# A GRU, a convolution and an expert layer on one core: the state h turned by VectorE in place of TensorE

## The chip, the cores and the metric

The kernel runs on one core of a Trainium2 chip. The metric is the device time of one execution in microseconds; a run's time is the median of several executions. A profile is one further execution with the hardware profiler on; its own time stands beside its span below.

## What is computed

The reference, cut to what matters. x is (128, 64, 512): 128 sequences (B), 64 steps (T), 512 features (D); the condition is (128, 512).

```python
def cell(h, x):                                  # GRU: 64 steps, one after the other
    gi = x @ W_ih + b_ih                         # 512 -> 3 * 512
    gh = h @ W_hh + b_hh
    i_r, i_z, i_n = split(gi, 3); h_r, h_z, h_n = split(gh, 3)
    r = sigmoid(i_r + h_r); z = sigmoid(i_z + h_z)
    n = tanh(i_n + r * h_n)
    return (1 - z) * n + z * h

hs = scan(cell, cond, x)
x = x + hs @ (ternary(weight) * scale).T + bias  # "ffn", ternary weights
y = causal_depthwise_conv(x, taps=cond) + b      # 64 taps per feature
x = x + y_experts(y) + shared_expert(y)          # top 6 of 64 experts, capacity 64
```

All inputs and outputs are float32.

## The kernel before

The program has two halves. The first, which the change is in, walks through the 64 steps of the GRU (some 1230 of the 2465 us); the second makes the convolution, the shared expert and the routed experts, and is left as it is.

The batch lies on the 128 partitions: the state `h`, the gates and `n` are tiles of 128 x 512. For the products TensorE needs h with the features on the partitions, so each step turns h: `turned_up` (L412) makes four 128x128 transposes on TensorE against an identity into one PSUM tile, `pst`. The full-precision product is made of three products on reduced operands: `split_h` (L419) cuts the low bits of the turned h (`hcut`, L344, VectorE), copies that (`hh`, L424, ScalarE), takes the rest (`hl`, L350, VectorE) and a mixture of both (`hs`, L351, VectorE). `split_x` (L367) does the same to the next step's input x, but there the rest, `xl`, is taken by GpSimd (L350 on POOL), followed on GpSimd by the addition of the ffn's bias (L286). Weights are split once, at the start.

The loop (L569) goes over t. In each turn TensorE makes, in an order that a scheduler settles when the kernel is built:

- nine groups of four products with hh, hl and hs: the gates' state parts (`psx`, `psy`: r; `psw`, `psz`: n; `psa`, `psb`: z),
- two groups of the ffn of the step before (`psf`, hh and hl with the ternary weights),
- six groups of the next step's input parts of n and r (`psw`, `psz`, `psx`, `psy`),
- the four transposes of the new h (L416),
- three groups of the next step's input part of z (`psa`, `psb`).

VectorE and ScalarE make the gates meanwhile (`cell_r`, `cell_n`, `cell_z`, L471 to L506; L506 writes the new h), then VectorE gathers the next step's input part of n (`gi`, L391 and L392), and then comes the cut of the turned h. Every engine executes its own queue in order. The gates r and z share one tile, `rz`, of the pool `el0` with one buffer; so do hcut, hh, hl and hs each.

Steps 0 to 3 are special: their turned h is also stored, since the ternary weights are ready only in step `LATE` = 4 (`ternary`, L448), and the ffn of these four steps is made up for in steps 6, 9, 12 and 15 (`late_ffn`, L551: it cuts a loaded h, and adds two groups to TensorE's turn). In step 4 the ternary weights are made on VectorE (L466, L467), after the gates.

`next_inputs` (L530) is where the turn is asked for:

```python
            if t in postponed:
                late_ffn(postponed[t])
            turned = turned_up(h)
            ...
            if t > 0:
                pieces = split_h(turned)
            input_gate(t + 1, 1)
```

After the loop the last h is turned once more by `turned_up`, for the last ffn.

Of the kernel before, what the change touches and what calls it, by code (L numbers as in the profile page):

```python
# [8 lines left out]
F32 = mybir.dt.float32  # L9
# [10 lines left out]
P = 128  # L20
B = 128
T = 64
D = 512
KD = D // P
# [21 lines left out]
def adaln_ffn_kernel(  # L46
# [22 lines left out]
    nc = tc.nc  # L69
# [139 lines left out]
    with (  # L209
# [46 lines left out]
        LATE = 4  # L256
# [38 lines left out]
        h = el0.tile([P, D], F32, name="h")  # L295
# [31 lines left out]
        def banks(c):  # L327
            pool = ps_gh if c == 1 else ps_gi
            return [pool.tile([P, D], F32, name=n) for n in BANKS[c]]
# [13 lines left out]
        def masked(dst, src):  # L343
            return nc.vector.tensor_scalar(  # L344
                dst.bitcast(I32), src.bitcast(I32), LOW, None, ALU.bitwise_and
            )

        def low_parts(engine, lo, mix, full, cut):

            i = engine.tensor_sub(lo, full, cut)  # L350
            nc.vector.scalar_tensor_tensor(mix, lo.bitcast(F32), -SPLIT, cut, ALU.mult, ALU.add)  # L351
            return i
# [26 lines left out]
        def input_gate(t, c):  # L379

            xh, xl, xs = parts_of[t]
            wh, wl, ws = wih[c]
            a, b = banks(c)
            products(a, xh, wh, start=True)
            products(a, xl, wl, stop=c == 2 or c in PLAIN.get(t, ()))
            products(b, xs, ws, start=True, stop=c == 2)
            if c != 2:
                gis[t, c] = a, b
                return
            g = el0.tile([P, D], F32, name="gi")  # L390
            nc.vector.scalar_tensor_tensor(g, a, WHOLE, bin_, ALU.mult, ALU.add)  # L391
            nc.vector.tensor_add(g, b, g)  # L392
            gis[t, c] = g
# [18 lines left out]
        def turned_up(src):  # L412
            ps = ps_f.tile([P, D], F32, name="pst")
            ps = ps.rearrange("p (k b) -> p k b", k=KD)
            for k in range(KD):
                nc.tensor.transpose(ps[:, k, :], src[:, k * P : (k + 1) * P], ident)  # L416
            return ps

        def split_h(ps, mixed=True):  # L419

            cut = el0.tile([P, KD, B], F32, name="hcut")
            hh, hl, hs = (el0.tile([P, KD, B], F32R, name=f"h{n}") for n in "hls")
            masked(cut, ps)
            nc.scalar.copy(hh, cut)  # L424
            if mixed:
                low_parts(nc.vector, hl, hs, ps, cut)
            else:
                nc.vector.tensor_sub(hl, ps, cut)
            return hh, hl, hs
# [80 lines left out]
        for c in (0, 2, 1):  # L510
            a, b = banks(c)
# [18 lines left out]
        def next_inputs(t):  # L530

            if t > 0:
                input_gate(t + 1, 2)
                input_gate(t + 1, 0)
            else:
                input_gate(1, 0)
                input_gate(1, 2)
            if t in postponed:
                late_ffn(postponed[t])
            turned = turned_up(h)  # L540
            hT = pieces = None
            if t < LATE:
                hT = io0.tile([P, KD, B], F32, name="xn")
                nc.scalar.copy(hT, turned)
                nc.sync.dma_start(out=htd[t], in_=hT.rearrange("p k b -> p (k b)"))
# [3 lines that stand above are left out]
            return pieces, hT  # L549

        def late_ffn(t):  # L551

            hh, hl = (el0.tile([P, KD, B], F32R, name=f"h{n}") for n in "hl")
            cut = el0.tile([P, KD, B], F32, name="hcut")
            full = hts.pop(t).rearrange("p (k b) -> p k b", k=KD)
            masked(cut, full)
            nc.scalar.copy(hh, cut)
            nc.vector.tensor_sub(hl, full, cut)
            ffn(t, (hh, hl))

        split_x(1)
        for c in (0, 2, 1):
            convert(raw_i[c], wih[c], stm)
        load_xt(2)
        pieces, hT = next_inputs(0)
        convert(raw_h[0], whh[0], stm)
        stage.close()

        for t in range(1, T):  # L569
# [28 lines left out]
            if t + 1 < T:  # L598
                pieces, hT = next_inputs(t)
            if t in (1, 2):  # L600
                c = 3 - t
# [38 lines left out]
        with tc.issue_after(grouped[-1].ins):  # L640
            turned = turned_up(h)
        early.append(conv_group(0, 3, ps_gi.tile([P, D], F32, name="psz")))
        pieces = split_h(turned, False)
        with tc.issue_after(grouped[-1].ins):
            ffn(T - 1, pieces)
# [1010 lines left out]
```

## Time and profile before

| what | value |
| --- | --- |
| median of 3 runs | 2467.7 us (2464.25 to 2468.32) |
| profiled execution: its own time | 2466.93 us |
| profiled execution: span from the first to the last instruction | 2465.2 us |
| granted TensorE clock | 0.998 |
| TensorE busy | 2450.6 us (99%) |
| VectorE busy | 1547.5 us (63%) |
| ScalarE busy | 462.6 us (19%) |
| GpSimd busy | 447.2 us (18%) |
| in the recurrence, 320 to 1215 us: TensorE, VectorE busy | 895.0 of 895.0 us, 642.2 us |

In the profile PE is TensorE, PEld its loading of weights, DVE VectorE, ACT ScalarE, POOL GpSimd, SP SyncE. A line such as L344 is the line of the kernel; helpers record all their callers' work under their own line, so hcut, xcut and the cuts of the weights are all L344. In a timeline the columns are start and length in us, then what ran; an "x4" is four instructions merged into one row, and brackets give the engine's idle time ahead of it and who ended it. In a list of groups the columns behind the first bar are the sum in us and the mean of one in ns, behind the second the idle time ahead of them. Matmuls overlap: a row's length is more than the distance to the next row.

### The profile page before, as it was taken

The page shows a single profiled execution, that of the slowest core. Times are in us where ns is not written, and L with a number is a line of the kernel's source. Part 1 is how long each engine was busy: PE and PEld are TensorE (multiplying, and loading weights), DVE is VectorE, ACT ScalarE, POOL GpSimd, SP SyncE. Part 2 cuts the span into 40 slices and gives each one's busy share as a digit, 9 for nine tenths or more (in the row PEclk, how much of TensorE's full clock was granted, in tenths as well). Part 3 has the DMA queues.
Part 4 walks back from the last instruction along what each step waited for, and adds up shares of the span by engine and source line. Part 5 has one row for each costly group of instructions (what it writes and reads, how often), then busy time and mean ns, then how long its engine had stood idle before and what let it go on. Part 6 is the DMA issues. An engine that isn't in the chain of part 4 may idle for free.

```text
span 2465.2 us, 32121 instructions
## 1 busy us (share of the span) xinstructions
PE 2450.6 (99%) x12317; PEld 1886.5 (77%) x12317; DVE 1547.5 (63%) x3073; ACT 462.6 (19%) x847; POOL 447.2 (18%) x468
## 2 busy tenths in 40 slices
PE   9999999999999999999999999999999999999999
PEld 5788888888888888888896678888876666666667
DVE  8877777777777777677686566666664333443344
ACT  5211111111111111111122222222211111111111
POOL 1122221112111211221220000000011222222220
PEclk9999999999999999999999999999999999999999
DMA  5244443233222222222498212222368999899961
GB/s 182 74 87 80 82 80 62 58 68 63 60 54 59 59 52 55 61 56 43 111 336 295 39 25 40 56 58 62 103 173 288 299 299 311 267 334 292 290 172 44
DMA packets 464456, 322.33 MB, mean 131 GB/s; under 512 B 316592, under 2 KB 384176, under 8 KB 462128
## 3 DMA queue, kind: packets, MB, share of 16 engines
q1 hardware_dynamic: 435408, 246.34, 34.8%
q0 software_dynamic: 28896, 73.95, 13.2%
q8 instruction: 97, 1.59, 0.3%
q14 instruction: 55, 0.45, 0.1%
HBM read 233.44 MB, written 92.03 MB: 132 GB/s over the span
## 4 chain that ended last, share of the span: by engine, by line
PE 97%; DVE 1%; issue 1%; DMA 0%; ACT 0%; POOL 0%; DVEq 0%; SPq 0%; ACTq 0%; POOLq 0%
PE psa L333 9%; PE psw L333 9%; PE psx L333 9%; PE psw L815 8%; PE psx L815 8%; PE psz L815 8%; PE psy L333 5%; PE psb L333 5%; PE psf L333 5%; PE psz L333 5%; PE y L815 4%; PE py L1541 3%; PE pg L1515 3%; PE pu L1515 3%; PE y L992 2%; PE psc L191 2%
## 5 line engine op out<-in xcount | busy, mean ns | idle before, releaser
L1525 DVE SCALAR_TENSOR_TENSOR a<-a,rw,pu 128x352 f32<-128x352 f32 x32 | 18.6, 581 | 213.0 <-PE pu L1515 213.0
L351 DVE SCALAR_TENSOR_TENSOR xs<-xl,xcut 128x512 fp32r<-128x512 f32 x63 | 103.4, 1641 | 68.1 <-POOL xl L350 68.1
L344 DVE TENSOR_SCALAR hcut<-pst 128x512 int32<-128x512 int32 x63 | 43.5, 690 | 130.9 <-PE pst L416 128.7
L1097 POOL DMA_DIRECT2D out_dram<-hid x32 | 27.7, 1006 | 449.6 <-issue 333.6
L350 POOL TENSOR_TENSOR xl<-xp,xcut 128x512 fp32r<-128x512 f32 x60 | 83.4, 1391 | 141.9 <-PE psa L333 141.7
L479 ACT ACTIVATE rz<-rz 128x512 f32<-128x512 f32 x64 | 40.5, 633 | 341.6 <-DVE rz L478 341.6
L424 ACT CAST hh<-hcut 128x512 fp32r<-128x512 f32 x63 | 39.2, 622 | 341.9 <-DVE hcut L344 341.9
L268 POOL DMA_DIRECT2D q<-in_x_dram x36 | 19.3, 537 | 419.1 <-DMA out_dram<-q 202.1
L1541 PE MATMUL py<-wd,aeT 128*64 128x512 f32 (+1 forms) x384 | 88.8, 597 | 0.0
L1515 PE MATMUL pg<-wg,xeT 128*64 128x352 f32 x512 | 81.2, 459 | 0.0
L1515 PE MATMUL pu<-wu,xeT 128*64 128x352 f32 x512 | 81.2, 459 | 0.0
L1552 POOL DMA_INDIRECT out_dram<-ys,idxo x32 | 45.5, 1422 | 179.8 <-DMA out_dram<-ys,idxp 161.1
L1552 POOL DMA_INDIRECT out_dram<-ys,idxp x32 | 46.3, 1448 | 174.3 <-DMA out_dram<-ys,idxo 85.1
L268 POOL DMA_DIRECT2D xn<-in_x_dram x28 | 15.0, 536 | 325.6 <-DMA out_dram<-xn 176.2
L333 PE MATMUL psa<-wih1h,xh 128*128 128x512 f32 x252 | 73.9, 414 | 0.0
L1515 PEld LDWEIGHTS pg<-wg,xeT 128*64 128x64 f32 x512 | 36.5, 136 | 47.2 <-issue 46.6
L492 ACT ACTIVATE n<-n 128x512 f32<-128x512 f32 x64 | 40.5, 633 | 165.6 <-DVE n L491 163.2
L855 ACT ACTIVATE g<-psx 128x256 f32<-128x256 f32 x80 | 30.7, 383 | 217.6 <-DVE aT L862 158.5
L333 PE MATMUL psf<-sgn,hl 128*128 128x512 f32 x256 | 70.1, 397 | 0.0
L333 PE MATMUL psf<-sgn,hh 128*128 128x512 f32 x256 | 69.5, 393 | 0.3 <-ACT hh L424 0.3
L333 PE MATMUL psw<-wih2h,xh 128*128 128x512 f32 x252 | 68.7, 395 | 0.0
L333 PE MATMUL psa<-wih1l,xl 128*128 128x512 f32 x252 | 68.6, 394 | 0.0
(404 smaller groups left out, 6183.3 us busy)
## 6 DMA issues: line engine op xcount, KB each, us to landing
wg<-in_w_gate_dram SPq DMA_DIRECT2D x64, 704.0 KB, 12.1
wu<-in_w_up_dram SPq DMA_DIRECT2D x64, 704.0 KB, 12.5
wd<-in_w_down_dram SPq DMA_DIRECT2D x64, 512.0 KB, 9.9
xc<-x1c SPq DMA_DIRECT2D x32, 512.0 KB, 6.6
xp<-in_xT_dram POOLq DMA_DIRECT2D x62, 256.0 KB, 3.0
tab<-hid SPq DMA_DIRECT2D x56, 256.0 KB, 4.3
wd<-in_w_down_dram SPq DMA_DIRECT2D x64, 192.0 KB, 9.8
q<-in_x_dram POOLq DMA_DIRECT2D x36, 256.0 KB, 2.9
```

Source lines behind the costliest of these rows:

```text
L191: i = nc.tensor.matmul(ps[rows, j].rearrange("p h (u t) -> p h u t", u=2), xcs[sl % NCB][:, rows, g * 4 + j], tzs[sl % NCB][:, :, :, g * 4 ...
L333: i = nc.tensor.matmul(ps, lhs[:, k, :], rhs[:, k, :], start=start and k == 0, stop=stop and k == KD - 1, skip_group_check=True,)
L344: return nc.vector.tensor_scalar(dst.bitcast(I32), src.bitcast(I32), LOW, None, ALU.bitwise_and)
L350: i = engine.tensor_sub(lo, full, cut)
L351: nc.vector.scalar_tensor_tensor(mix, lo.bitcast(F32), -SPLIT, cut, ALU.mult, ALU.add)
L479: nc.scalar.activation(r, r, AF.Sigmoid)
L492: nc.scalar.activation(n, n, AF.Tanh)
L815: i = nc.tensor.matmul(ps.rearrange("p (j b) -> p j b", b=P) if len(r.shape) == 3 else ps, lhs(k), r, start=(first and k == 0), stop=(k == ...
L992: nc.tensor.matmul(gu.rearrange("p (j b) -> p j b", b=P), swr[:, k].rearrange("p w n -> p (w n)"), rows[:, k], start=(k == 0), stop=(k == ...
L1515: nc.tensor.matmul(acc[halves[j]], self.xeT[:, k, halves[j]], self.ws[j][which][:, k, :], start=(k == 0), stop=(k == KD - 1),)
L1541: nc.tensor.matmul(py[halves[j]], self.aeT[:n, c, halves[j]], self.ws[j][2][:n, c, :], start=(c == 0), stop=(c == len(ech) - 1),)
L1552: nc.gpsimd.indirect_dma_start(out=out, out_offset=bass.IndirectOffsetOnAxis(ap=(idxp[:CAP] if j == 0 else idxo)[:, q : q + 1], axis=0), i ...
```

## The change

From step 4 on the turn is made by `turned_over` instead of `turned_up`: sixteen VectorE transposes, each of a 32-partition block of h with four blocks of 32 columns, 128 columns apart. Each writes one 32-partition block of the turned tile. The turned h lies in the tile `rz` of the gates (SBUF) instead of `pst` (PSUM). As built, the first transpose stands between L391 and L392 in VectorE's queue and the other fifteen behind L392, ahead of the cut; TensorE's queue is the same but for the four transposes less; in step 4 seven transposes are interleaved with the making of the ternary weights, and xs of the next input stands ahead of the cut. The changed file has 12 lines more from L419 on, so that its line numbers lie 12 higher behind there.

```diff
+        Q = 32
+
+        def turned_over(src):
+
+            dst = el0.tile([P, D], F32, name="rz").rearrange("p (k b) -> p k b", k=KD)
+            rows = src.rearrange("b (k j c) -> b k j c", k=KD, c=Q)
+            for j in range(P // Q):
+                for i in range(B // Q):
+                    own, new = slice(i * Q, (i + 1) * Q), slice(j * Q, (j + 1) * Q)
+                    nc.vector.transpose(dst[new, :, own], rows[own, :, j, :])
+            return dst
+
...
-            turned = turned_up(h)
+            turned = turned_over(h) if t >= LATE else turned_up(h)
```

## The prediction

> **What bounds the kernel now.** I read the page's shares first, then the chain that ended last, then one steady step of the recurrence on each engine, then the waits of the recurrence (320 to 1215 us).
>
> ```profile
> PE 2450.6 (99%) x12317; PEld 1886.5 (77%) x12317; DVE 1547.5 (63%) x3073; ACT 462.6 (19%) x847; POOL 447.2 (18%) x468
> ...
> PE 97%; DVE 1%; issue 1%; DMA 0%; ACT 0%; POOL 0%; DVEq 0%; SPq 0%; ACTq 0%; POOLq 0%
> ```
>
> TensorE is never out of work: less work for it is worth its full time, but only until another engine makes it wait. So the question is how much room the recurrence leaves. One step, TensorE first, then VectorE (start, length, what; in brackets the idle time before):
>
> ```profile
> 1023.95 1.08 PE L333 MATMUL psy<-wih0s,xs 128*128 128x512 f32 x4
> 1024.87 0.60 PE L416 MATMUL pst<-ident,h 128*128 128x128 f32 x4
> 1025.22 1.17 PE L333 MATMUL psa<-wih1h,xh 128*128 128x512 f32 x4
> 1026.23 1.09 PE L333 MATMUL psa<-wih1l,xl 128*128 128x512 f32 x4
> ...
> 1028.07 1.08 PE L333 MATMUL psx<-whh0h,hh 128*128 128x512 f32 x4
> ```
>
> ```profile
> 1021.00 0.69 DVE L506 TENSOR_TENSOR h<-h,n 128x512 f32<-128x512 f32 x1
> 1021.61 0.68 DVE L391 SCALAR_TENSOR_TENSOR gi<-psw,bin 128x512 f32<-128x512 f32 x1
> 1022.40 0.69 DVE L392 TENSOR_TENSOR gi<-psz,gi 128x512 f32<-128x512 f32 x1
> 1025.51 0.69 DVE L344 TENSOR_SCALAR hcut<-pst 128x512 int32<-128x512 int32 x1 [2.42 <-PE pst L416]
> ```
>
> h is ready at 1021.69, but TensorE turns it only at 1024.87, behind the next step's input products: VectorE idles 2.42 us. The first product that needs the turned h (psx, 1028.07) has not to wait. The previous psx began at 1009.20, so a step lasts 18.87 us. Below, times are from that psx.
>
> **The change, part by part.** Step 4 to step 62 are changed: 59 turns; the last one (t = 63) stays.
>
> *Removed:* four transposes of 128x128 per turn. They start 0.35 us before psa, and psa's first group takes 1.01 us where a group usually takes 0.91: 0.45 us of TensorE per step, all on the bounding engine. Without a wait the step would be 18.42 us.
>
> *Added:* sixteen VectorE transposes of 32 partitions x 128 elements. The built order puts the first between the two gi lines and fifteen behind the second, all ahead of the cut. No row shows such an instruction. The nearest is a copy of 128 elements, the next a pair of tiny copies that go to different halves of the partitions:
>
> ```profile
> L1533 DVE COPY aeT<-py 96x128 f32<-96x128 f32 x32 | 8.9, 278 | 0.0
> ...
> L1502 DVE COPY rw<-rows 64x1 f32<-64x1 f32 x64 | 9.1, 143 | 0.5
> ```
>
> The same pair in the timeline, start and length of both together:
>
> ```profile
> 1838.81 0.30 DVE L1502 COPY rw<-rows 64x1 f32<-64x1 f32 x2
> ```
>
> The pair takes 0.30 us, the sum of its two durations: no overlap where the partitions change, and each transpose reads another block of partitions than the one before. So I take 0.278 us each, without overlap. Lower bound: 0.20 us, what lies between the start of that 128-element copy (1923.54) and the next instruction (1923.74) where the partitions stay. Upper bound: 0.42 us, a 256-element row (L849: 424 ns), if an element costs two passes. [...]
>
> *Where they lie:* h is ready at 12.49; the second gi, 0.06 us later for the transpose ahead of it, ends at 13.95. Fifteen times 0.278 is 4.17: the cut is asked for at 13.95 + 4.17 + 0.03 = 18.15, where it starts at 16.31 today. The 2.42 us of idle time hide only part.
>
> *Moved operand:* hcut (L344) and hl (L350) read PSUM today, and will read the gates' tile in SBUF. hcut alone gets shorter: 0.43 us (xcut, from SBUF) for 0.69. But hl gets two SBUF inputs, and GpSimd is at work just then: its xl follows psa's second group (18.21 today, 17.76 without the transposes) for 1.30 us, to 19.06, with the bias addition of 1.29 behind it. A cut from SBUF under these two is in the trace (four postponed steps):
>
> ```profile
> 249.93 1.39 POOL L350 TENSOR_TENSOR xl<-xp,xcut 128x512 fp32r<-128x512 f32 x1 [0.63 <-PE psa L333]
> 251.28 1.47 POOL L286 TENSOR_TENSOR q<-q,fb 128x512 f32<-128x512 f32 x1
> ...
> 250.25 1.34 DVE L344 TENSOR_SCALAR hcut<-q 128x512 int32<-128x512 int32 x1
> 251.52 1.77 DVE L351 SCALAR_TENSOR_TENSOR xs<-xl,xcut 128x512 fp32r<-128x512 f32 x1
> ```
>
> Asked for during xl, the cut takes 1.34 us instead of 0.43 and ends 0.27 after xl; the two-input xs behind it ends 0.54 after the addition. [...]
>
> *Sum of a step:* the cut ends at 19.06 + 0.27 = 19.33. ScalarE's hh follows (0.03 + 0.62), TensorE starts 0.05 later and its first group takes 0.11 more after a wait (1232.26 in the trace: 0.05 behind hh, 1.03 us for 0.92). 19.33 + 0.81 = 20.14: 1.27 us longer. hl, blocked by the addition, ends about 21.05 and is needed at 21.99; hs is 21.8 for 22.9; xs and xcut end about 23.0, where psx lets the next r start (23.1): all just covered. What is queued on VectorE behind the transposes is thus late but, except hcut, not too late.
>
> Four of the 59 steps also carry a postponed feed-forward: 1.86 us more of TensorE ahead of psa. There the transposes are mostly covered: between -0.2 and +1.3 each, 2 us together. In step 4 the ternary weights' eight VectorE lines (1.96 + 3.0 us) are interleaved with the transposes (4.45), and xs is put ahead of the cut (0.68): h at 110.6, cut ended at 121.1, psx at 122 for 114.8: 7 us once. The other 54: 54 x 1.27 = 68.6. In all 77.6 us on the profiled execution's 2466.9 (span 2465.2 and 1.7 around it): 2544.5. The median of the runs is 0.8 above that execution: 2545.
>
> **The rivals.**
> *Faster: the transposes overlap.* At 0.20 us each the cut is asked for at 16.98, ahead of xl; hcut ends at 17.41, hl starts before GpSimd, hh is there at 18.1 and TensorE (18.42) never waits. 54 x -0.45 = -24, step 4 still +6: 2449. It needs transposes under 0.22 us; even is 0.243 (13.95 + 15d + 0.03 + 0.43 + 0.81 = 18.87). For it: independent 512-element lines start 0.08 us before the one ahead has ended. Against: the pair above.
> *Slower by twice: the cut waits for the bias addition too*, because the transposes take over 0.338 us (asked for after 19.06), or as at 191.79. It ends 0.3 after 20.35, psx at 21.46: 2.59 a step, 54 x 2.59 + 9 = 149: 2616.
> *No wait at GpSimd at all:* 18.15 + 0.43 + 0.81 = 19.39: 0.52 a step, 28 + 9: 2504. Against it: of the four cuts of hcut from SBUF three took 1.34 to 3.18 us, and at the fourth (0.43) GpSimd was idle.
> At 0.42 us and more each the transposes end after the addition and set the step alone: 21.5 and up, over 2630.
>
> **How the numbers follow.** Forecast 0.50, slow rival 0.25, no wait 0.11, faster 0.08, over 0.42 us 0.04, near the even point 0.02. The range takes in the three slower cases with their own few microseconds, 2500 to 2630; the faster one and the tail lie outside. Slower by over 0.2% (about 5 us, what a measurement of this kernel can tell) is 0.90, faster 0.08, same 0.02.
>
> **What would show it.** Right: TensorE idle about 1.6 us before psx <- whh0h, ended by hh, in nearly each step; transposes of some 0.28 to 0.31 us end to end; hcut from rz at about 1.2 us, hl from rz near 1.7; step 20.1 us; TensorE's clock unchanged. Wrong: no idle before psx (the faster rival), hcut at 0.43 (no wait), hcut above 2 us or transposes over 0.34 us (the slow one).

## The result, and the profile after

The changed kernel takes 2602.9 us (median of 4 runs, 2600.07 to 2613.03) where the kernel before takes 2466.9 (4 runs): 1.0558 times the time, 95% interval 1.0545 to 1.057. The forecast of slower holds, and the range (2500 to 2630) holds the time; the forecast time itself, 2545, is 58 us too low. The profiled execution took 2613.03 us, span 2611.3, granted TensorE clock 0.982 for 0.998.

The page's shares and the chain that ended last: TensorE, never out of work before, now idles for 5% of the span, and a fifth of the chain is VectorE.

```profile
PE 2475.7 (95%) x12081; PEld 1881.7 (72%) x12081; DVE 1825.8 (70%) x4017; ACT 467.8 (18%) x847; POOL 446.1 (17%) x468
...
PE 74%; DVE 20%; issue 3%; ACT 1%; DMA 1%; POOL 0%; DVEq 0%; SPq 0%; POOLq 0%; ACTq 0%
```

The page's groups of the change (behind the first bar the sum in us and the mean in ns, behind the second the idle time before and who ended it):

```profile
L428 DVE STREAM_TRANSPOSE rz<-h 32x128 f32<-32x128 f32 x944 | 285.3, 302 | 12.2
L333 PE MATMUL psx<-whh0h,hh 128*128 128x512 f32 x248 | 84.1, 466 | 121.4 <-ACT hh L436 121.4
...
L350 DVE TENSOR_TENSOR hl<-rz,hcut 128x512 fp32r<-128x512 f32 x59 | 77.6, 1315 | 1.9
...
L344 DVE TENSOR_SCALAR hcut<-rz 128x512 int32<-128x512 int32 x59 | 70.9, 1202 | 2.0
```

944 transposes are 59 turns of 16. All of TensorE's new idle time, 121.4 us, lies ahead of psx and is ended by hh, where the forecast put it. In the timeline a regular step looks like this: TensorE, then VectorE, then GpSimd.

```profile
1065.01 1.19 PE L333 MATMUL psx<-whh0h,hh 128*128 128x512 f32 x4 [1.45 <-ACT hh L436]
...
1082.68 1.07 PE L333 MATMUL psb<-wih1s,xs 128*128 128x512 f32 x4
1085.19 1.19 PE L333 MATMUL psx<-whh0h,hh 128*128 128x512 f32 x4 [1.45 <-ACT hh L436]
```

```profile
1079.06 4.74 DVE L428 STREAM_TRANSPOSE rz<-h 32x128 f32<-32x128 f32 x15
1083.83 0.66 DVE L344 TENSOR_SCALAR hcut<-rz 128x512 int32<-128x512 int32 x1
1084.52 1.64 DVE L350 TENSOR_TENSOR hl<-rz,hcut 128x512 fp32r<-128x512 f32 x1
```

```profile
1082.07 0.54 POOL L268 DMA_DIRECT2D xn<-in_x_dram  x1 [16.13 <-DMA out_dram<-xn]
1082.93 1.28 POOL L350 TENSOR_TENSOR xl<-xp,xcut 128x512 fp32r<-128x512 f32 x1 [0.33 <-PE psa L333]
1084.17 1.44 POOL L286 TENSOR_TENSOR q<-q,fb 128x512 f32<-128x512 f32 x1
```

From psx to psx it is 20.18 us, forecast 20.14. Fifteen transposes take 4.74, 0.316 from start to start; the cut is asked for at 18.82 of the step and ends at 19.48, 0.28 after xl. But not all steps are like that. A long one, with GpSimd, the cut and TensorE together:

```profile
434.00 0.54 POOL L268 DMA_DIRECT2D q<-in_x_dram  x1 [17.55 <-DMA out_dram<-q]
434.32 3.02 DVE L344 TENSOR_SCALAR hcut<-rz 128x512 int32<-128x512 int32 x1
434.56 1.27 POOL L350 TENSOR_TENSOR xl<-xp,xcut 128x512 fp32r<-128x512 f32 x1
435.77 1.27 POOL L286 TENSOR_TENSOR xn<-xn,fb 128x512 f32<-128x512 f32 x1
...
438.04 2.08 PE L333 MATMUL psx<-whh0h,hh 128*128 128x512 f32 x4 [3.85 <-ACT hh L436]
...
439.92 1.91 PE L333 MATMUL psw<-whh2h,hh 128*128 128x512 f32 x4
441.62 1.91 PE L333 MATMUL psx<-whh0l,hl 128*128 128x512 f32 x4
...
444.38 1.10 PE L333 MATMUL psw<-whh2l,hl 128*128 128x512 f32 x4
```

Two things differ. GpSimd's load of x (L268) came late, because it waits for the store that frees its buffer; it stands ahead of xl in GpSimd's queue, so xl started late, straight behind the load. The cut, asked for during the load, ended 0.30 us behind the addition: 3.02 us. In the whole trace, all 17 cuts beside an xl that started straight behind its load waited for xl and the addition (2.17 to 3.16 us); all 36 beside an xl that had itself waited for TensorE ended 0.28 us behind xl (0.61 to 0.71 us). Why the cut gets in between there is not shown: in the rows the addition follows xl without a gap in both cases. And after the wait of 3.85 us the products take 1.91 us a group for 1.10. Busy times in 2 us stretches (the last three numbers are granted clock, DMA share and GB/s) show the clock halved for six microseconds:

```profile
437.00:439.00 2.00, 0.96 (x2) 0.83 (x3) 1.93 (x4) 0.62 (x1) 0.54 (x2) 0.50 0.29 115
439.00:441.00 2.00, 2.00 (x6) 1.55 (x5) 0.82 (x2) 0.00 (x0) 0.00 (x0) 0.50 0.04 16
441.00:443.00 2.00, 2.00 (x6) 1.52 (x6) 0.00 (x0) 0.00 (x0) 0.00 (x0) 0.50 0.00 0
443.00:445.00 2.00, 2.00 (x9) 1.64 (x8) 1.11 (x2) 0.00 (x0) 0.00 (x0) 0.85 0.00 0
```

The whole difference of the profiled executions is 2613.03 - 2466.93 = 146.1 us. By steps of the timeline:

| part | forecast | profiled |
| --- | --- | --- |
| regular steps: 54 x 1.27; 53 x 1.28 | 68.6 | 67.8 |
| steps with a late ffn | 2 | -0.6 |
| step 4 and the two behind it | 7 | 16.6 |
| 16 steps with a long cut and the last turn, what goes beyond 1.45 us of wait | - | 30.3 |
| halved clock behind these waits | - | 29.1 |
| outside these steps | - | 2.6 |
| sum | 77.6 | 145.8 |

The median of the runs is 10 us below this execution.

### The profile page after: what moved, and what is told of

Read it like the earlier page. It is cut to its first block, busy times and chain, and to the rows that moved or that the text cites. A ratio compares the mean times of both kernels' runs of the same rounds, so it can differ in the third digit from the quotient of the medians.

```text
span 2611.3 us, 32486 instructions
## 1 busy us (share of the span) xinstructions
PE 2475.7 (95%) x12081; PEld 1881.7 (72%) x12081; DVE 1825.8 (70%) x4017; ACT 467.8 (18%) x847; POOL 446.1 (17%) x468
## 4 chain that ended last, share of the span: by engine, by line
PE 74%; DVE 20%; issue 3%; ACT 1%; DMA 1%; POOL 0%; DVEq 0%; SPq 0%; POOLq 0%; ACTq 0%
DVE rz L428 10%; PE psw L827 7%; PE psz L827 7%; PE psx L827 7%; PE psx L333 6%; PE psw L333 5%; PE psa L333 5%; PE psf L333 5%; PE y L827 4%; PE py L1553 3%; PE psy L333 3%; PE pg L1527 3%; PE pu L1527 3%; PE psb L333 3%; PE psz L333 3%
## 5 line engine op out<-in xcount | busy, mean ns | idle before, releaser
L428 DVE STREAM_TRANSPOSE rz<-h 32x128 f32<-32x128 f32 x944 | 285.3, 302 | 12.2
L333 PE MATMUL psx<-whh0h,hh 128*128 128x512 f32 x248 | 84.1, 466 | 121.4 <-ACT hh L436 121.4
L333 PEld LDWEIGHTS psx<-whh0h,hh 128*128 128x128 f32 x248 | 47.4, 212 | 152.9 <-ACT hh L436 145.8
L268 POOL DMA_DIRECT2D q<-in_x_dram x36 | 19.3, 537 | 504.9 <-DMA out_dram<-q 478.8
L374 ACT CAST xh<-xcut 128x512 fp32r<-128x512 f32 x63 | 39.2, 623 | 328.8 <-PE psa L333 328.5
L489 DVE SCALAR_TENSOR_TENSOR rz<-psx,br 128x512 f32<-128x512 f32 x63 | 43.5, 690 | 65.0 <-PE psx L333 64.6
L268 POOL DMA_DIRECT2D xn<-in_x_dram x28 | 15.0, 536 | 398.2 <-DMA out_dram<-xn 362.5
L333 PE MATMUL psw<-whh2h,hh 128*128 128x512 f32 x248 | 80.0, 451 | 0.0
L350 DVE TENSOR_TENSOR hl<-rz,hcut 128x512 fp32r<-128x512 f32 x59 | 77.6, 1315 | 1.9
L333 PE MATMUL psx<-whh0l,hl 128*128 128x512 f32 x248 | 77.7, 440 | 0.0
L344 DVE TENSOR_SCALAR hcut<-rz 128x512 int32<-128x512 int32 x59 | 70.9, 1202 | 2.0
L333 PE MATMUL psy<-whh0s,hs 128*128 128x512 f32 x248 | 71.2, 410 | 0.0
```

The source lines that it names most:

```text
L333: i = nc.tensor.matmul(ps, lhs[:, k, :], rhs[:, k, :], start=start and k == 0, stop=stop and k == KD - 1, skip_group_check=True,)
L344: return nc.vector.tensor_scalar(dst.bitcast(I32), src.bitcast(I32), LOW, None, ALU.bitwise_and)
L374: nc.scalar.copy(xh, cut)
L428: nc.vector.transpose(dst[new, :, own], rows[own, :, j, :])
L489: nc.vector.scalar_tensor_tensor(r, a, WHOLE, br, ALU.mult, ALU.add)
```

## The experiments

My theory after the comparison: a regular step is as forecast; GpSimd's late load makes 17 of the cuts long; a long wait halves TensorE's clock in the next step. The rivals: the long cuts come from the bias addition alone, or from the gates' tile in SBUF; the slow products are a side effect of memory traffic, and follow no wait.

**One: the load of x on the Sync queue**, so that this load no longer stands ahead of xl on GpSimd.

```diff
-            nc.gpsimd.dma_start(out=xns[t], in_=x[:, t, :])
+            nc.sync.dma_start(out=xns[t], in_=x[:, t, :])
```

> The changed kernel, but the loads of x for the feed-forward (L268) are issued by SyncE's queue and no longer by GpSimd's. Theory (in 17 of the steps GpSimd's load came late, xl and the bias addition followed it without a gap, and the cut hcut had to wait for both; the loss of clock follows from that): xl starts by TensorE alone, hcut takes about 0.65 us in every regular step, the step is 20.15 us throughout, no clock below 1.0 behind step 6; 2466.9 + 68 + 16 = about 2550 us (2543 to 2560). Rival (the long cuts have another cause, such as where the cut falls within xl): still 15 or more cuts over 2 us and about 2600 us.

2550.8 us (2549.4 to 2552.3), 1.0342 of before (1.0325 to 1.036), as expected. TensorE's waits by line in the recurrence (sum, times, longest), which are step 4's, 53 of 1.45 to 1.50 us and the last turn's 2.9 (in the changed kernel the last turn's cut takes 2.05 us, beside GpSimd's clearing of buffers for the convolution, L122):

```profile
PE psx L333 <- ACT hh L436: 90.1, 55, 10.3
```

One queue's load made 52 of the 136 us: the long cuts, and with them the halved clock (granted clock of this run 0.996). What is left is the kernel that the prediction describes, and it forecast 2545 for it.

**Two: the bias addition left out**; the late load stays.

```diff
-                        nc.gpsimd.tensor_add(xns[t], xns[t], fb)
+                        pass
```

> The changed kernel without the bias addition on GpSimd (L286 left out: the feed-forward lacks its bias). [...] Rival (GpSimd has nothing to do with it, the long steps are VectorE's own): about 2600 us.

My estimate without the addition, with cuts that end 0.27 us behind xl at the latest as at 250.25 in the trace of before: 2550 to 2560 us, waits under 2.3 us, no loss of clock behind step 6, and hl near 0.7 us in place of 1.64.

2564.5 us (2563.2 to 2566.7), 1.0399 (1.0382 to 1.0416): well below the rival's 2600, but 4 us above my range; hl is 0.69 us as estimated, the waits and the clock are not. Waits are 1.45 in most steps, but 1.55 to 2.62 in thirteen: a late xl alone still holds the cut. Behind waits of 2.10, 2.61 and 2.61 the next step lost 1.5 us to the clock; behind two others of 2.61 and 2.62 nothing. The addition is one of the two causes of a long cut; it takes a late load to put it in the way.

**Three: the transposes made and not used**; TensorE turns h as before, and the cut reads PSUM.

```diff
-            turned = turned_over(h) if t >= LATE else turned_up(h)
+            if t >= LATE:
+                turned_over(h)
+            turned = turned_up(h)
```

> The sixteen transposes are made as in the changed kernel, but not used: TensorE's four transposes stay and the cut reads PSUM. Theory (the transposes cost their place in VectorE's queue in every step, the source in SBUF costs the long steps and thereby the clock): the cut is asked for at the same place, takes 0.69 us in every step, steps of 20.2 us, no loss of clock behind step 6; about 2555 us (2545 to 2565). Rival one (the queue alone makes all of the 136 us): about 2600 us. Rival two (the source in SBUF makes most of it): 2467 to 2500 us.

2552.3 us (2551.7 to 2553.8), 1.0346 (1.0328 to 1.0363), as expected. One cut, the xl that starts beside it, and the psx that follows:

```profile
1059.03 0.69 DVE L344 TENSOR_SCALAR hcut<-pst 128x512 int32<-128x512 int32 x1
1059.37 1.28 POOL L350 TENSOR_TENSOR xl<-xp,xcut 128x512 fp32r<-128x512 f32 x1
...
1060.43 1.19 PE L333 MATMUL psx<-whh0h,hh 128*128 128x512 f32 x4 [1.02 <-ACT hh L436]
```

The cut takes 678 to 693 ns in all 63 steps: with PSUM as its source it is not blocked, also where xl runs. Yet the step is 20.18 us, the same as in the changed kernel. So in a regular step the wait does not need the block at all: the transposes alone bring the cut to 18.8 of the step, and its 0.69 us from PSUM end where 0.43 from SBUF and 0.23 of blocking end.

**Four: four unused products** behind psb, which keep TensorE busy in the wait.

```diff
+            if t >= LATE:
+                spare = ps_f.tile([P, D], F32, name="pst")
+                products(spare, parts_of[t + 1][2], wih[1][2], start=True, stop=True)
```

> The changed kernel with one unused group of four products on TensorE behind psb in each step (0.92 us, into the bank that the transposes had). Theory (a wait of about 3 us halves TensorE's clock, one of 1.45 us does not): waits become 0.5 and 2.1 us, cuts stay as long as they were, the granted clock stays at 1.0 in most steps; 2603 - 29 = about 2575 us (2565 to 2585), faster with more work. Rival (the clock's loss does not come from the wait, or costs nothing): 2600 us or above.

2592.7 us (2587.2 to 2593.4), 1.0511 (1.0494 to 1.0529): 18 us off my number. The wait fell by 0.9 us to 0.55, but from step 6 on there were still eleven long ones, of 2.1 to 2.9, and behind six of these some 1.5 us was lost (2.7 behind the longest). So a filler of 0.9 us is too short; that the clock answers to the wait was still only likely, and experiments seven and eight test it.

**Five: transposes that stay in their 32 partitions.** The kernel leaves out the exchange of blocks between the partition groups, so that h is not fully turned.

```diff
-                    nc.vector.transpose(dst[new, :, own], rows[own, :, j, :])
+                    nc.vector.transpose(dst[new, :, own], rows[new, :, i, :])
```

> Each of the sixteen transposes of a step reads and writes the same 32 partitions, four in a row for each group of 32 partitions, where the changed kernel reads another group with each instruction; the blocks of h so come from other rows, so this part of the computation is changed and the rest stays. The theory that a transpose overlaps the next one where both stay in the same partitions (the faster rival's mechanism in the prediction) expects a spacing of 0.20 to 0.24 us for twelve of the sixteen, the cut asked for 1.0 to 1.4 us earlier, most of the wait of 1.45 us gone, and 2500 to 2540 us. The theory that transposes follow one another without overlap whatever partitions they use expects the spacing of 0.316 us of the changed kernel and its time, 2590 to 2610 us.

2475.2 us (2470.8 to 2476.3), 1.0028 (1.0019 to 1.0038): 25 us below even the range of the overlap theory. In the timeline, a step with psx at 965.49 and 983.95:

```profile
979.38 3.37 DVE L428 STREAM_TRANSPOSE rz<-h 32x128 f32<-32x128 f32 x15
982.78 0.46 DVE L344 TENSOR_SCALAR hcut<-rz 128x512 int32<-128x512 int32 x1
```

The same instructions on the same number of elements, 0.225 us apart on average for 0.316, and 128 us of the changed kernel's time are gone, most of the long cuts among them: what it lacked was the overlap. In the changed kernel, where each transpose reads another group of 32 partitions than the last, all 820 that follow directly on another start 13 to 14 ns behind its end; here, at 0.272 us each in the mean and 0.225 apart, they overlap; a change of the output's group alone was not run. The faster rival's mechanism is thus real, and its step nearly: the cut asked for at 17.29, ahead of xl, no wait for hh, 18.46 us here and 18.50 in the median. The time misses that rival's 2449 because steps 4 to 6 still cost 9 us, three steps ahead of a late ffn had waits of 3 us and then a halved clock (15 us), and the regular steps come to 8 us more than at 18.42.

**Six: the load on Sync, and the two gi lines behind the cut**; the turn begins with step 5.

```diff
-            gis[t, c] = g
+            if t > LATE:
+                return gather
+            gather()
...
+            if between is not None:
+                with tc.issue_after(i.ins):
+                    between()
```

> The load of x moved to the Sync queue (the first experiment, 2550.8 us), and the two VectorE additions that gather the next step's input for the n gate (0.65 us each) moved from ahead of the transposes and between them to behind the cut; the turn over VectorE begins with step 5 in place of step 4. Theory that the wait is the cut standing behind xl: the transposes end at about 17.6 us of the step, ahead of xl (17.8), the cut is done at 18.0, and the step takes 18.9 to 19.3 us in place of 20.15: 62 steps less 0.85 to 1.25 give 2470 to 2498 us. Rival, that the length of VectorE's own chain decides and the moved additions come back behind the cut in front of hl: no more than half of the 0.85 us is won, 2520 to 2551 us.

2474.7 us (2472.4 to 2476.8), 1.0032 (1.0021 to 1.0044), as expected. VectorE and GpSimd of one step:

```profile
988.86 5.05 DVE L433 STREAM_TRANSPOSE rz<-h 32x128 f32<-32x128 f32 x16
993.94 0.43 DVE L344 TENSOR_SCALAR hcut<-rz 128x512 int32<-128x512 int32 x1
994.28 0.68 DVE L392 SCALAR_TENSOR_TENSOR gi<-psw,bin 128x512 f32<-128x512 f32 x1
```

```profile
994.10 1.41 POOL L350 TENSOR_TENSOR xl<-xp,xcut 128x512 fp32r<-128x512 f32 x1 [15.32 <-PE psa L333]
```

The transposes are as slow as ever, but the cut starts 0.16 us ahead of xl and takes 0.43. The wait falls from 1.45 to 0.21, and nearly all the loss is gone (some 11 of the 76 us won against experiment one are step 4's, which TensorE turns here): it was a matter of what stood ahead of the cut in the queue.

**Seven and eight: longer waits.** On experiment one's kernel the last four, or the last eight, transposes are made twice.

```diff
-            for j in range(P // Q):
+            for j in (0, 1, 2, 3, 3):          # eight: (0, 1, 2, 3, 2, 3)
```

> On the first experiment's kernel (load of x on the Sync queue, 2550.8 us, a TensorE wait of 1.45 us in each step) the last four transposes of a step are made twice. By the sum the wait grows by 4 x 0.316 = 1.26 to 2.7 us and 58 steps take 73 us more: 2624 us, if the clock of TensorE does not answer to the wait. Theory that waits of 2.6 us and more bring the clock down in the next step in part of the cases: groups of products at 1.9 us in place of 1.1 after some of these waits, 10 to 60 us above that sum.

> On the first experiment's kernel (2550.8 us) the last eight transposes of a step are made twice. By the sum the wait grows by 8 x 0.316 = 2.53 to 4.0 us and 58 steps take 147 us more: 2698 us, if the clock of TensorE does not answer to the wait. Theory that a wait of about 3 us and more brings the clock down in the next step: the products after nearly every wait run at 1.9 us a group for a while, 1.5 to 2.9 us lost in each of 58 steps, 2780 to 2870 us.

2669.8 us (2669.3 to 2670.5) and 2806.3 us (2805.0 to 2810.5): 46 and 108 above the sums without a clock effect, both within what the clock theory expected. Three steps running with four more, the wait the same each time; the first two of its products after each:

```profile
997.16 1.31 PE L333 MATMUL psx<-whh0h,hh 128*128 128x512 f32 x4 [2.67 <-ACT hh L436]
998.27 1.91 PE L333 MATMUL psw<-whh2h,hh 128*128 128x512 f32 x4
...
1020.03 1.19 PE L333 MATMUL psx<-whh0h,hh 128*128 128x512 f32 x4 [2.67 <-ACT hh L436]
1021.06 1.10 PE L333 MATMUL psw<-whh2h,hh 128*128 128x512 f32 x4
...
1041.37 1.19 PE L333 MATMUL psx<-whh0h,hh 128*128 128x512 f32 x4 [2.67 <-ACT hh L436]
1042.40 1.86 PE L333 MATMUL psw<-whh2h,hh 128*128 128x512 f32 x4
```

Behind a wait of 2.67 us nearly every second step loses 1.5 us (22 of the last 45: steps of 21.4 and 22.9 in turn). Behind 4.0 us every one of the last 43 loses 1.2 to 1.6, or 2.8 (seven of them). Behind 1.45 us (experiment one) none does. Four-more's granted clock (third number from the right), DMA share and GB/s in a slow stretch and in the full-speed stretch of the next step:

```profile
999.00:1001.00 2.00, 2.00 (x6) 1.51 (x6) 0.00 (x0) 0.00 (x0) 0.00 (x0) 0.50 0.00 0
1021.00:1023.00 2.00, 2.00 (x10) 1.61 (x10) 0.60 (x2) 0.00 (x0) 0.00 (x0) 1.00 0.12 47
```

The slow stretch has no memory traffic at all, the other has some: what slows the products is the halved clock, not traffic. Why every second wait of 2.67 us brings it and the others don't is not shown.

**Nine to twelve: can the VectorE turn win?** From experiment six on: hh copied in two halves and the bias addition placed beside the transposes (nine); the ffn's VectorE line moved from ahead of h's last two lines to behind hs (ten); ten with TensorE's turn in all steps (eleven); and ten with hh in one piece and h - n placed behind the z gate's second line (twelve). The edits, in this order, cut to what matters, with comments added:

```diff
-            nc.scalar.copy(hh, cut)
+            for k in range(2):
+                nc.scalar.copy(hh[:, k * HK : (k + 1) * HK], cut[:, k * HK : (k + 1) * HK])
...
-                add_bias(t + 1, last_low)
+                with tc.issue_after(last_low.ins):
+                    i = nc.gpsimd.tensor_copy(tick, h[:, :1])
+                add_bias(t + 1, i)
...
+            while later:                       # finish() holds ffn's last lines
+                with tc.issue_after(i.ins):
+                    later.pop()()
...
-            nc.vector.tensor_sub(h, h, n)      # in cell_n
+            with tc.issue_after(i.ins):        # in cell_z, i: its second line
+                nc.vector.tensor_sub(h, h, n)
```

> On the kernel with the gather behind the cut (2474.7 us, step 18.93 with a wait of 0.21 us), two more edits: hh is copied on ScalarE in two halves of 256 elements, so that the first products can start on the first half; and the bias addition on GpSimd is placed, with a tiny copy of h ahead of it, beside the transposes in place of behind xl. Theory: the wait of 0.21 us and its refill stood on the chain cut, hh, products; the half copy takes 0.3 us off that chain and TensorE sets the step with the 18.43 us that the steps without a wait took in the run with transposes within one block of partitions: 62 x 0.4 = 25 us less, and 10 us less in the four steps with a late ffn: 2440 to 2460 us. Rival: VectorE, busy for all but 0.46 us of that step, sets it, and the step stays within 0.1 us: 2465 to 2475 us.

> As the run with the two halves, and the VectorE line of ffn moved from ahead of h's last two lines to behind hs; it waited there 0.46 us for psf, and h's last lines behind it. Theory: h is final 0.36 us earlier and TensorE, without a wait, sets the step at 18.43 us: 2440 to 2455 us, below the run with the two halves by 0 to 10 us. Rival: the line comes back ahead of xs and the next step's chain: 2455 to 2475 us.

> All edits of the run with ffn behind, but with TensorE's four transposes in all steps. If the edits around the turn bring nothing where TensorE sets the step, it takes what the kernel before takes, 2455 to 2470 us (up to 10 us less, since the late ffn steps lose some cover), and the difference to the run before it is the price of the turn on TensorE, 58 x 0.45 = 26 us at most.

> On the run with ffn behind (2465.6 us, step 18.70): hh is copied in one piece again (the first products waited little for it, and the three steps ahead of the VectorE turn had grown from 17.2 to 17.8 us with the halves), and the subtraction h - n on VectorE is placed behind the second line of the z gate instead of ahead of it. Theory: in that run the second z line starts 1.0 us after TensorE has finished psb, because VectorE is still at h - n, and VectorE then stands 0.76 us idle for z's sigmoid; with the two lines changed round the sigmoid starts about 0.6 us earlier, h, the transposes and the cut come 0.6 us earlier, TensorE has no wait and sets the step at 18.43 to 18.5 us: 58 x 0.4 us below the kernel before, 2438 to 2450 us. Rival: the step is held by something else (the head of the step on TensorE, or VectorE's total of 18 us), and stays at 18.6 to 18.8 us: 2455 to 2467 us.

| kernel | median us | ratio to before (95%) | regular step |
| --- | --- | --- | --- |
| nine | 2461.1 | 0.9975 (0.9965 to 0.9984) | 18.77 |
| ten | 2465.6 | 0.9992 (0.9983 to 1.0001) | 18.70 |
| eleven (TensorE's turn) | 2479.1 | 1.0047 (1.0033 to 1.0062) | 18.97 |
| twelve | 2453.8 | 0.9946 (0.9933 to 0.996) | 18.49 |

Nine missed its 2440 to 2460 by a microsecond. Ten missed its 2440 to 2455: its step stayed at 18.7, and its time can't be told from the kernel before. Eleven missed its 2455 to 2470: the edits cost TensorE's own version 11.5 us instead of nothing. Ten and eleven differ in the turn alone, and there the VectorE turn is 13 us ahead. In ten the timeline of VectorE showed what held the step:

```profile
972.32 0.69 DVE L535 TENSOR_TENSOR rz<-psb,rz 128x512 f32<-128x512 f32 x1
973.76 0.69 DVE L537 TENSOR_TENSOR h<-h,rz 128x512 f32<-128x512 f32 x1 [0.76 <-ACT rz L536]
```

With the z gate's line ahead of h - n, twelve has no wait, and the step is 18.47:

```profile
955.23 1.08 PE L334 MATMUL psx<-whh0h,hh 128*128 128x512 f32 x4
...
972.80 1.07 PE L334 MATMUL psb<-wih1s,xs 128*128 128x512 f32 x4
973.70 1.08 PE L334 MATMUL psx<-whh0h,hh 128*128 128x512 f32 x4
```

Twelve beats both kernels, by 13.5 us against before. Its order with TensorE's turn was not run, so how much of this is the turn's is known for ten's order only. It still misses its 2438 to 2450, and its timeline says where:

```profile
1211.28 1.98 PE L191 MATMUL psx<-tz,xc 128*64 128x128 f32 x16 [5.29 <-DMA tz<-tzd]
```

Behind the loop TensorE waits 5.29 us for a load of the convolution's taps (ten has 5.67 there, eleven 4.37, nine and the kernel before none). Nine and ten differ in the place of the ffn line and its stores alone, so the wait comes with them. How is read from the trace: the load stands on the Sync queue behind the stores of ffn's output, which the later line puts back; they are issued 1.8 us after the last psx in twelve, 7.7 us ahead of it before. Nine's place for the ffn line with twelve's order was not tried.

## Why the prediction was right or wrong

*The range:* that 2500 to 2630 holds 2602.9 is partly luck. It reached that far for a slow rival in all steps; what carried the time there was that rival in some steps and a clock that the prediction took as unchanged.

*Removed, 0.45 us a step:* right within 0.1. Steps without a wait take 18.50 us (five) and 18.49 (twelve) in the median for the 18.42 of the sum.

*Transposes, 0.278 us without overlap:* right in kind (five), 0.302 in size and 0.316 from start to start. The row of the trace was 12% low; the 0.31 us that closes my range for them stands on no run, and these two were measured. It changed nothing: at 18.15 or 18.82 the cut ends behind xl.

*The cut ends 0.27 after xl, psx at 20.14:* measured 0.28 and 20.18. But the weight of the two causes was otherwise. I had the cut asked for 0.9 us before xl's end and blocked for the rest; it was asked for 0.4 us before it and blocked for 0.23. Three shows that a cut from PSUM, with no block, gives a step as long; without the block a cut from SBUF would have ended 0.23 us earlier. hcut's median, 660 ns, is accordingly half of the 1.2 us that I named as the sign; that the page's mean is 1202 ns is chance, a mean of short cuts and long ones.

*hl blocked but covered:* right, 1.64 us in the regular step, and no product waits for it.

*The slow rival as an alternative:* this is the step that failed. I took "the cut waits for the addition too" as another state of all steps, with a chance of 0.25, and the forecast as free of it. Both occur in one execution: 16 regular steps waited for both, 28.8 us (the last turn's 1.5 us of the 30.3 is the clearing of buffers, not this). The trace of before had shown one of four such cuts at 3.18 us, and I did not ask what made that one differ. The answer lay in GpSimd's queue, which I did not read beyond xl: the load ahead of it waits for a store, and when it comes late, xl starts straight behind it. The trace of before shows this at the cut of 3.18 us (191.79, the row that the slow rival names), while at the two of 1.34 xl had waited for TensorE:

```profile
191.58 0.54 POOL L268 DMA_DIRECT2D q<-in_x_dram  x1 [14.15 <-DMA out_dram<-q]
192.13 1.31 POOL L350 TENSOR_TENSOR xl<-xp,xcut 128x512 fp32r<-128x512 f32 x1
193.38 1.29 POOL L286 TENSOR_TENSOR xn<-xn,fb 128x512 f32<-128x512 f32 x1
...
191.79 3.18 DVE L344 TENSOR_SCALAR hcut<-q 128x512 int32<-128x512 int32 x1
```

*"TensorE's clock unchanged":* wrong, and worth 29.1 us. I priced the wait at its length. That holds for the waits of 1.45 us, and not for most of those of 3 us. Without these two, experiment one's 2550.8 is 6 us above the forecast.

*Step 4, 7 us:* 9.9 us in the step itself, as VectorE's lines there took longer than summed (two of the ternary lines 1.05 and 1.30 us for 0.49 and 0.75, beside GpSimd's xl and addition, and a blocked cut of 1.48 at the end); then a halved clock behind its wait of 10.26 us and one more wait of 4.03: 16.6 in all.

*The faster rival's "under 0.22 us":* five came to 0.225 and removed the wait, so the bound was about right; what it lacked was a way to keep the partitions. Moving lines from ahead of the cut (six) was a way that the prediction did not see: it took the built order as given.

## What to carry to other kernels

An instruction that replaces work on a bounding engine is paid for in the queue it joins (here fifteen transposes, 4.74 us ahead of the cut): ask which lines stand ahead of the one that everybody waits for, and whether they need to. Two outcomes that depend on when a neighbour's instruction starts are not alternatives for the whole run; they mix from step to step (17 long cuts and 36 short ones here), and each has to be counted. A wait of TensorE had two prices in these runs, its length and, in part of the cases from 2.08 us on (experiment four, the shortest with a fall; up to 1.81 us, in experiment two, there was none), the clock behind it: 0.50, and 1.2 to 2.9 us lost.

## What the runs showed of the hardware that I had not expected

- The granted TensorE clock fell to 0.50 behind waits (437 to 443 us in the changed kernel, 999 to 1001 us in experiment seven), and the shortest wait with slow products behind it, 1.81 and 1.91 us a group for 1.10, was 2.08 us (experiment four). Not every wait did this: behind none of the waits of 1.45 us in experiment one, behind half of those of 2.67 in experiment seven, behind 13 of 16 of 2.97 to 3.85 in the changed kernel, behind all of 4.0 in experiment eight. A fall cost 1.2 to 2.9 us.
- A cut from SBUF that was asked for early in an xl which started straight behind its load, or already during that load, waited for xl and the addition (2.17 to 3.16 us, 17 of 17 in the changed kernel); where xl had itself waited for TensorE, the cut got in between (0.61 to 0.71, 36 of 36). The 36 were asked for 0.85 to 0.95 us after xl had begun, the 17 at most 0.62 us after. A cut from PSUM was not blocked (678 to 693 ns, 63 of 63 in experiment three).
- Sixteen transposes in a row are 5.05 us where each reads another block of 32 partitions than the last (experiment six); where four in a row stay in the same block they are 0.225 us apart on average (experiment five).
